# A state-space scan, attention and experts on one core: other scan inputs from ScalarE, softplus in one place, a minimum with an operand per partition

## The chip, the cores and the metric

The kernel runs on one core of a Trainium2 chip. The metric is the time of one execution on the device, in microseconds (us). The time before is the median of three runs. A separate execution was profiled, and the traces and tables below are of that one.

The engines are called by these names: PE (TensorE, with PEld for its weight loads), DVE (VectorE), ACT (ScalarE), POOL (GpSimd) and SP (SyncE, which issues the DMAs).

## The reference

Two layers work on four images of 384 channels by 32 x 32 positions, all in 32-bit floats.

Layer 0 is a selective scan. An image is normalised by groups. For each of four directions `k` (rows, columns, and both reversed) it is projected to a step width `dt`, to `B` and to `C`. Each channel then carries 16 states along the 1024 positions:

```python
dt = jax.nn.softplus(dts.astype(jnp.float32) + dt_projs_bias...[None, :, :, None])
...
dA = jnp.exp(dtt[..., None] * A)
h = h * dA + (dtt * ut)[..., None] * bt[:, :, None, :]
y = jnp.einsum('bkdn,bkn->bkd', h, ct)
```

The four directions are merged and normalised, put through gelu and added to the image.

Layer 1 sees an image as 1024 tokens of 384 channels. A causal attention (softmax of the scores, whose maximum is subtracted) is added. Then a mixture of four experts is added, of which the two likeliest count for each token. The reference computes all four experts, and so does the kernel.

## The kernel before

**Units and ticks.** The scan is cut into 768 units, 192 for each image. A unit holds 32 channels times 4 states on the 128 partitions and 1024 positions along the free dimension. A group is four units (`NJ`) that share their `B` and `C` rows; a block is four groups (`EACH`, 16 units), one direction of 128 channels. The program is written out by a planner, a loop over ticks (lines 1393 to 1422), with one unit a tick. At tick `t` it writes, in this order:

- on ScalarE, the decay `da` of unit `t + 2` (an exponential, line 552; three buffers);
- on VectorE, the scan's input `v = du * B` of unit `t` (`front`, line 559), where it was not made otherwise. `v` lies in PSUM and has two buffers;
- on TensorE, the transposes that make `v` of unit `t + 1` in the other way (`turned`, line 860);
- on POOL, the product of the states of unit `t - 1` with `C` (`back`, line 572), which is ordered behind the VectorE multiply of the same tick;
- work that was put off to this tick, among it `softmax` (line 1008), which stands between the multiply and the scan;
- on VectorE, the scan of unit `t` (`middle`, line 565);
- on TensorE, in every fourth tick, 16 matmuls that sum a group's states into `y` (`row`, line 597);
- DMA loads for units ahead (`fetch`), then one step of the preparation of an image (`preparation`), then the side jobs and as much attention or experts of the image before as a budget allows (`go_on`).

Each engine works through its own queue in this order.

**The other way to a scan input.** In the first image, TensorE and ScalarE are free of attention and experts. There the side job `feed` (lines 776 to 850) prepares the inputs of whole groups. It loads `du` of a block again (line 808). TensorE transposes four 128 x 128 pieces into a PSUM bank (`dut`, line 815), and then the other four. ScalarE copies each piece four times, with a state's `B` as the scale per position (32 instructions a group, line 838), into a buffer `st`. Of these there are two. `turned` transposes back into `v` when the group's units come. A group takes five ticks, eight scalings in each of four. It is left out if it can't be started five ticks before its first unit (`AHEAD`), and a unit whose `st` is not there in time takes the VectorE multiply. A group doesn't start before the one two before it has been consumed (lines 822 to 824). Before the change the second and the fourth group of each block are candidates (line 818).

**Softplus.** `project_dt` (lines 409 to 446) computes `dt` of 128 channels for two directions. In each half of the positions two matmuls fill two PSUM banks, and in a later tick two softplus empty them (line 431). In the first image there are only two such banks, and `feed` uses the same ones. Softplus and the exponential of `da` need different ScalarE tables, so that the change between them is an `ACT_TABLE_LOAD`. Ten such projections fall in the first image's ticks, five for it and five for the second image.

**Softmax.** `scores` makes one or two pieces of 128 rows of scores, already negated, so that the row's minimum `nb` takes the maximum's place. Where there are two pieces, their two minima are combined at line 1016. ScalarE's exponential then reads the result as its bias. `normalise` adds the two exponent sums (line 1028). In each image four of eight row blocks have two pieces.

Of the kernel before, what the change touches and what calls it, by code (L numbers as in the profile page):

```python
# [10 lines left out]
ALU = mybir.AluOpType  # L11
# [22 lines left out]
NQ = N // NI  # L34
NJ = P // DJ
# [7 lines left out]
AHEAD = 5  # L43
# [6 lines left out]
def hybrid_kernel(  # L50
# [22 lines left out]
    nc = tc.nc  # L73
# [37 lines left out]
    clock = [-100]  # L111
# [3 lines left out]
    def defer(ticks, f, where=due):  # L115
        where.setdefault(clock[0] + ticks, []).append(f)
# [176 lines left out]
    def columns(v):  # L293

        return v.rearrange("p (h w) -> p w h", w=HW)
# [113 lines left out]
    def project_dt(b, pair, m, u, xd):  # L409

        ks = PAIRS[pair]
        while not slots.ready(3 + pair):
            yield "wait", 1
        v = u[m]
        if pair == 1:
            v = slots.now(f"ut_{b}_{m}", P, L)
            nc.scalar.copy(v.rearrange("p (w h) -> p w h", h=HW), columns(u[m]))
        dts = [slots.now(f"dt_{b}_{k}_{m}", P, L) for k in ks]
        for h in range(NH):
            while not banks.ready(2):  # L420
                yield "wait", 1
            pss = [banks.now(f"pdt_{b}_{k}_{m}_{h}") for k in ks]
            for i, k in enumerate(ks):
                r = slice(64 * pair + 32 * i, 64 * pair + 32 * i + R)
                nc.tensor.matmul(  # L425
                    pss[i], wdt[r, m * P : (m + 1) * P], xd[r, bass.ts(h, 512)],
                    start=True, stop=True,
                )
            yield "wait", 1
            for i, k in enumerate(ks):  # L430
                nc.scalar.activation(  # L431
                    dts[i][:, bass.ts(h, 512)], pss[i], AF.Softplus, bias=dtb[:, k, m : m + 1]
                )
                banks.give(f"pdt_{b}_{k}_{m}_{h}")
        yield "wait", 1
        for i, k in enumerate(ks):
            nc.sync.dma_start(dts_d[b, k][0, m * P : (m + 1) * P, :], dts[i])
            du = yield from slots.take(f"du_{b}_{k}_{m}", P, L)
            nc.vector.tensor_mul(du, dts[i], v)
            yield "wait", 1  # L440
            nc.sync.dma_start(dts_d[b, k][1, m * P : (m + 1) * P, :], du)
            if b == 0:
                stored_du.add((k, m))
            slots.give(f"dt_{b}_{k}_{m}", f"du_{b}_{k}_{m}")
        if pair == 1:
            slots.give(f"ut_{b}_{m}")

    EACH = NQ * NJ
    IMAGE = M * K * EACH
# [326 lines left out]
    def feed():  # L776
        bt = one.tile([P, 2, NT, 4 * N], F32, tag="fx0", name="bt")

        def turn_rows(pair):
            while pair not in stored_rows:  # L780
                yield "wait", 1
            rows = yield from slots.take(f"bt_{pair}", 4 * N, L)
            nc.sync.dma_start(rows, rows_d[0, pair].rearrange("k j n l -> (k j n) l"))
            yield "wait", 2
            ps = yield from banks.take(f"pbt_{pair}")
            for t in range(NT):
                nc.tensor.transpose(
                    ps[:, t * 4 * N : (t + 1) * 4 * N], rows[:, t * P : (t + 1) * P],
                    ident[: 4 * N, : 4 * N],
                )  # L790
            yield "wait", 1
            nc.scalar.copy(bt[:, pair], ps.rearrange("p (t n) -> p t n", t=NT))
            banks.give(f"pbt_{pair}")
            slots.give(f"bt_{pair}")

        begun = []
        yield from turn_rows(0)
        for n in range(0, IMAGE, EACH):
            u = units[n]
            if clock[0] > n + EACH - NJ - AHEAD:  # L800
                continue
            if u["pair"] == 1 and u["m"] == 0 and u["i"] == 0:
                yield from turn_rows(1)
            while (u["k"], u["m"]) not in stored_du:
                yield "wait", 1
            name = f"turn_{u['name']}"
            du = yield from slots.take(name, P, L)
            nc.sync.dma_start(du, dts_d[0, u["k"]][1, u["m"] * P : (u["m"] + 1) * P, :])
            yield "wait", 2

            def dut(q, h, du=du, name=name):
                ps = banks.now(f"{name}_{q}_{h}")
                for t in range(4):
                    o = (4 * h + t) * P
                    nc.tensor.transpose(ps[:, t * P : (t + 1) * P], du[:, o : o + P], ident)
                return ps

            for q in range(1, NQ, 2):
                n0 = n + q * NJ
                if clock[0] > n0 - AHEAD:  # L820
                    continue
                while len(begun) >= 2 and clock[0] < begun[-2] + NJ:

                    yield "wait", 1
                if clock[0] > n0 - AHEAD:
                    continue
                begun.append(n0)
                st = pools["st"].tile([P, NT, NJ * P], F32, tag="st", name=f"st_{n0}")
                ps = [None, None]
                for h in range(2):  # L830
                    if ps[h] is None:
                        while not banks.ready():
                            yield "wait", 1
                        ps[h] = dut(q, h)
                        yield "wait", 1
                    for t in range(4):
                        for i in range(NI):
                            nc.scalar.activation(  # L838
                                st[:, 4 * h + t, :].rearrange("p (d i) -> p i d", i=NI)[:, i, :],
                                ps[h][:, t * P : (t + 1) * P], AF.Copy,  # L840
                                scale=bt[:, u["pair"], 4 * h + t, u["i"] * 2 * N + q * NI + i :][:, :1],
                            )
                        if t == 1:
                            if h == 0 and banks.ready():
                                ps[1] = dut(q, 1)
                            yield "wait", 1
                    banks.give(f"{name}_{q}_{h}")
                    yield "wait", 1
                scaled[n0] = st
            slots.give(name)  # L850
# [91 lines left out]
    def attention(b, yb, fx0):  # L942
# [65 lines left out]
        def softmax(i, ss, pr):  # L1008
            nb = sm.tile([P, 4], F32, tag="nb", name=f"nb_{b}_{i}")
            if alone:  # L1010
                ps = ss[-1][2][:, -P:]
                nc.vector.tensor_add(ps, ps, causal)
            for n, (o, e, ps) in enumerate(ss):
                nc.vector.tensor_reduce(nb[:, n : n + 1], ps, AX.X, ALU.min)  # L1014
            if len(ss) == 2:
                nc.vector.tensor_tensor(nb[:, 0:1], nb[:, 0:1], nb[:, 1:2], ALU.min)
            for n, (o, e, ps) in enumerate(ss):
                nc.scalar.activation(  # L1018
                    pr[:, o:e], ps, AF.Exp, bias=nb[:, 0:1], scale=-1.0,
                    accum_out=nb[:, 2 + n : 3 + n],  # L1020
                )
                banks.give(f"ss_{b}_{i}_{o}")
            defer(1, lambda: normalise(i, nb, len(ss)))

        def normalise(i, nb, n):
            wd = (i + 1) * P
            if n == 2:
                nc.vector.tensor_add(nb[:, 2:3], nb[:, 2:3], nb[:, 3:4])
            nc.vector.reciprocal(nb[:, 2:3], nb[:, 2:3])
            nc.scalar.activation(prs[i][:, :wd], prs[i][:, :wd], AF.Copy, scale=nb[:, 2:3])  # L1030

# [355 lines left out]
    clock[0] = -2  # L1387
    side.append(later())
    side.append(feed())
    decay(0)  # L1390
    decay(1)
# [85 lines left out]
```

## Time and profile before

| | |
|---|---|
| median of three runs | 3781.38 us (3779.78 to 3781.87) |
| the profiled execution | 3782.19 us, its span 3780.4 us |
| PE busy | 3348.6 us, 89% of the span |
| DVE busy | 2962.4 us, 78% |
| ACT busy | 2088.0 us, 55% |
| POOL busy | 1815.4 us, 48% |
| scans (line 565) | 768, 1750.6 us |
| multiplies for scan inputs (line 559) | 678, 840.6 us |
| scalings for scan inputs (line 838) | 736, 213.6 us |

The span runs from the first instruction to the last. In the slices of the page the span is cut into 40 equal parts of 94.5 us, and a digit is the busy share of a part in tenths. A line of the groups has the source line, engine, operation and tiles, the shapes and the count; then busy us and mean ns of one; then the idle time of the engine before them and what ended it. The busy time counts overlapping instructions once. A line of the timeline has the start and the length in us, the engine, the source line and the operation, with the number of instructions merged in it, and in brackets the idle time before it.

### The profile page before, as it was taken

Reading aid. Unit: us, or ns where it says so; the run is one execution under the profiler, and the core shown is the slowest. Engines: PE = TensorE matmul, PEld = TensorE weight load, DVE = VectorE, ACT = ScalarE, POOL = GpSimd, SP = SyncE. Lnnn points to the kernel's source line nnn. Section 1 sums busy time; section 2 is a strip of 40 time slices with the busy share of each in tenths; the row PEclk is TensorE's granted clock in tenths of the full one; section 3 lists DMA queues with packets and bytes.
Section 4 is the critical chain, followed back from the end, with each engine's and each line's share of the span. In section 5 each row is a group of like instructions: output and inputs, shape, how many; then the busy total and the mean of one; then the engine's idle time right before and its main releaser. Section 6 shows DMA issues by size and latency. Waiting matters only on the chain. (4 is left out here: it accounts for less than half of the span.)

```text
span 3780.4 us, 34707 instructions
## 1 busy us (share of the span) xinstructions
PE 3348.6 (89%) x11755; PEld 1523.6 (40%) x11755; DVE 2962.4 (78%) x2098; ACT 2088.0 (55%) x2754; POOL 1815.4 (48%) x776
## 2 busy tenths in 40 slices
PE   4666666689999999799999999889999998999999
PEld 1333323345343334345333344454344334644444
DVE  5899899988899899989988999999999992210000
ACT  5888888555666556556655555455554552322121
POOL 2777777545466556545555565455665660000000
PEclk7777876799999999898999999899999999999999
DMA  6656555635676757436666655455667551322321
GB/s 202 221 211 223 203 210 200 235 141 177 211 247 210 253 197 245 152 136 219 218 218 227 203 201 197 143 172 196 209 197 241 178 182 38 91 78 81 97 82 53
DMA packets 408017, 680.01 MB, mean 180 GB/s; under 512 B 33520, under 2 KB 279968, under 8 KB 407840
## 3 DMA queue, kind: packets, MB, share of 16 engines
q1 hardware_dynamic: 401632, 677.40, 52.6%
q8 instruction: 93, 1.52, 0.2%
q10 hardware_dynamic: 6208, 0.39, 0.1%
q14 instruction: 84, 0.69, 0.1%
HBM read 605.16 MB, written 72.55 MB: 179 GB/s over the span
## 5 line engine op out<-in xcount | busy, mean ns | idle before, releaser
L572 POOL TENSOR_TENSOR h<-h,bc 128x1024 f32<-128x1024 f32 x768 | 1814.3, 2367 | 1300.8 <-DVE v L559 1170.4
L565 DVE TENSOR_TENSOR_SCAN h<-da,v 128x1024 f32<-128x1024 f32 x768 | 1750.6, 2284 | 107.2 <-PE v L860 31.8
L552 ACT ACTIVATE da<-dt,a 128x1024 f32<-128x1024 f32 x768 | 882.8, 1156 | 916.0 <-DVE h L565 877.8
L1260 PE MATMUL ph<-fx,w 128*128 128x512 f32 x2304 | 1023.3, 600 | 3.5 <-DMA w<-in_w 2.0
L1285 PE MATMUL fy<-ht,w 128*128 128x512 f32 x2304 | 1022.4, 601 | 1.7 <-ACT dt L431 0.9
L559 DVE TENSOR_TENSOR v<-du,bc 128x1024 f32<-128x1024 f32 x678 | 840.6, 1240 | 35.0 <-DMA du<-dts 18.3
L1285 PEld LDWEIGHTS fy<-ht,w 128*128 128x128 f32 x2304 | 437.1, 192 | 575.9 <-issue 558.9
L1260 PEld LDWEIGHTS ph<-fx,w 128*128 128x128 f32 x2304 | 433.8, 191 | 578.6 <-issue 532.8
L597 PE MATMUL y<-h,sel 128*32 128x512 f32 x3072 | 489.7, 659 | 97.4 <-POOL h L572 97.2
L1245 ACT ACTIVATE ht<-ph,b1s 128x512 f32<-128x512 f32 x384 | 257.5, 678 | 463.3 <-PE ph L1260 462.5
L1294 DVE SCALAR_TENSOR_TENSOR fy<-fy,b2s,tw 128x512 f32<-128x512 f32 x96 | 72.4, 754 | 423.0 <-PE fy L1285 423.0
L597 PEld LDWEIGHTS y<-h,sel 128*32 128x32 f32 x3072 | 97.6, 116 | 407.4 <-issue 219.0
L860 PE MATMUL v<-ident,st 128*128 128x128 f32 x720 | 144.2, 366 | 112.7 <-DVE h L565 111.6
L838 ACT ACTIVATE st<-turn,bt 128x128 f32<-128x128 f32 x736 | 213.6, 532 | 0.1
L860 PEld LDWEIGHTS v<-ident,st 128*128 128x128 f32 x720 | 116.1, 190 | 158.3 <-DVE h L565 77.9
L1249 ACT ACTIVATE ht<-ht 128x3072 f32<-128x3072 f32 x64 | 176.9, 2764 | 0.8
L552 ACT ACT_TABLE_LOAD x108 | 138.6, 1283 | 15.5 <-DMA dt<-dts 11.8
L1067 PE MATMUL po<-pt,vt 128*128 128x256 f32 x480 | 110.2, 383 | 10.1 <-ACT pt L959 10.0
L425 PE MATMUL pdt<-xd,wdt 12*128 12x512 f32 x184 | 78.9, 753 | 33.4 <-ACT dt L431 24.7
L997 PE MATMUL ss<-axn,qt 128*128 128x512 f32 (+3 forms) x288 | 101.3, 497 | 7.7 <-ACT yb L1084 6.4
L1067 PEld LDWEIGHTS po<-pt,vt 128*128 128x128 f32 x480 | 96.0, 204 | 27.8 <-ACT pt L959 13.1
L997 PEld LDWEIGHTS ss<-axn,qt 128*128 128x128 f32 x288 | 50.5, 193 | 50.2 <-issue 30.0
(208 smaller groups left out, 1618.3 us busy)
## 6 DMA issues: line engine op xcount, KB each, us to landing
bc<-rows SPq DMA_DIRECT2D x384, 512.0 KB, 4.7
w<-in_w SPq DMA_DIRECT2D x384, 384.0 KB, 5.9
dt<-dts SPq DMA_DIRECT2D x192, 512.0 KB, 3.9
du<-dts SPq DMA_DIRECT2D x192, 512.0 KB, 6.5
dts<-dt SPq DMA_DIRECT2D x48, 512.0 KB, 3.6
dts<-du SPq DMA_DIRECT2D x48, 512.0 KB, 3.8
fx<-t2d SPq DMA_DIRECT2D x12, 768.0 KB, 5.8
tw<-mkd SPq DMA_DIRECT2D x32, 256.0 KB, 6.5
```

What stands on the lines that cost most here:

```text
L552: nc.scalar.activation(u["da"], spread["dt4", n], AF.Exp, scale=a4[:, g, u["q"] : u["q"] + 1])
L559: return nc.vector.tensor_tensor(u["v"], spread["du4", n], spread["bc", n][:, 0, :], ALU.mult)
L565: nc.vector.tensor_tensor_scan(u["h"][:, ::step], u["da"][:, ::step], u["v"][:, ::step], 0.0, op0=ALU.mult, op1=ALU.add,)
L572: product = nc.gpsimd.tensor_tensor(h, h, spread["bc", n][:, 1, :], ALU.mult)
L597: nc.tensor.matmul(y, sel, h, start=first, stop=last, tile_position=(0, jj * DJ))
L838: nc.scalar.activation(st[:, 4 * h + t, :].rearrange("p (d i) -> p i d", i=NI)[:, i, :], ps[h][:, t * P : (t + 1) * P], AF.Copy, scale=bt[ ...
L860: nc.tensor.transpose(u["v"][:, t * P : (t + 1) * P], st[:, t, u["j"] * P : (u["j"] + 1) * P], ident)
L1067: nc.tensor.matmul(pv[:, o:], vt[:, j, m * P : (m + 1) * P], pts[step][j // 4][:, j % 4, o:], start=(alone and j == 0), stop=(j == nj - 1),)
L1245: nc.scalar.activation(ht[:, f, :], ps, AF.Identity, bias=bias)
L1249: nc.scalar.activation(ht, ht, AF.Gelu)
L1260: nc.tensor.matmul(ps, tiles[n][:, c, (f % 2) * P : (f % 2 + 1) * P], xns[h][:, c, :], start=(c == 0), stop=(c == M - 1),)
L1285: nc.tensor.matmul(pss[m], tiles[n][:, f, :], hts[fh][:, f, :], start=(fh == 0 and f == 0), stop=(fh == 1 and f == FH - 1),)
```

## The change

Three edits. In `project_dt`, the wait of a tick between matmuls and softplus is left out for the second half of the positions, in the first image's ticks. In `feed`, all four groups of a block are looked at, and taken are those whose number in the image leaves 1, 3 or 4 when divided by five, in place of every second one. In the attention, two VectorE operations on 128 x 1 tensors take their second operand as a scalar per partition, and no longer as a tensor.

```diff
@@ project_dt
                     start=True, stop=True,
                 )
-            yield "wait", 1
+            if h == 0 or clock[0] >= IMAGE:
+
+                yield "wait", 1
             for i, k in enumerate(ks):
                 nc.scalar.activation(
                     dts[i][:, bass.ts(h, 512)], pss[i], AF.Softplus, bias=dtb[:, k, m : m + 1]
@@ feed
-            for q in range(1, NQ, 2):
+            for q in range(NQ):
                 n0 = n + q * NJ
-                if clock[0] > n0 - AHEAD:
+                if n0 // NJ % 5 not in (1, 3, 4) or clock[0] > n0 - AHEAD:
                     continue
                 while len(begun) >= 2 and clock[0] < begun[-2] + NJ:
@@ softmax
             if len(ss) == 2:
-                nc.vector.tensor_tensor(nb[:, 0:1], nb[:, 0:1], nb[:, 1:2], ALU.min)
+                nc.vector.tensor_scalar_min(nb[:, 0:1], nb[:, 0:1], nb[:, 1:2])
@@ normalise
             if n == 2:
-                nc.vector.tensor_add(nb[:, 2:3], nb[:, 2:3], nb[:, 3:4])
+                nc.vector.tensor_scalar_add(nb[:, 2:3], nb[:, 2:3], nb[:, 3:4])
```

## The prediction

> **What bounds the kernel now.** I read the page's slices first, then the windows by stage, then groups and waits of the first image (60 to 680 us, where nearly all of its 192 scan ticks lie), then single ticks in the timeline.
>
> ```profile
> PE   4666666689999999799999999889999998999999
> DVE  5899899988899899989988999999999992210000
> ACT  5888888555666556556655555455554552322121
> 60.00:680.00 620.00, 393.46 (x1804) 192.47 (x1804) 572.20 (x322) 513.80 (x1044) 450.86 (x190) 0.72 0.60 213
> 1300.00:1500.00 200.00, 198.31 (x613) 80.25 (x616) 182.00 (x126) 112.44 (x115) 111.87 (x48) 0.99 0.64 222
> 2455.00:2520.00 65.00, 54.02 (x251) 31.76 (x250) 63.78 (x58) 34.59 (x60) 32.97 (x14) 0.95 0.35 120
> ```
> The windows' columns are the stretch, its length, busy PE, PEld, DVE, ACT and POOL, then clock and DMA. Image 0 is VectorE's (572 of 620 us); ScalarE has 106 us free there. The experts are TensorE's (198 of 200). A softmax stretch of an attention (the third line) is VectorE's again, 63.8 of 65, and TensorE idles 11 us of it.
>
> Groups and waits of image 0:
>
> ```profile
> L565 DVE TENSOR_TENSOR_SCAN h<-da,v 128x1024 f32<-128x1024 f32 x190 | 429.9, 2281 | 47.4 <-PE v L860 31.8 <-DVE v L559 1.0 <-POOL h L572 0.9
> L838 ACT ACTIVATE st<-turn,bt 128x128 f32<-128x128 f32 x736 | 213.6, 532 | 0.1
> L559 DVE TENSOR_TENSOR v<-du,bc 128x1024 f32<-128x1024 f32 x99 | 126.2, 1275 | 0.3 <-DMA du<-dts 0.3
> L552 ACT ACT_TABLE_LOAD x21 | 26.9, 1283 | 0.4
> L431 ACT ACT_TABLE_LOAD x20 | 25.7, 1283 | 0.3
> ACT da L552 <- DVE h L565: 100.2, 80, 3.6
> ```
> 736 scalings in 32s are 23 groups fed by ScalarE. L559 runs 678 times in the program for 768 units, so 90 units have no VectorE multiply and 102 of image 0's 192 have. VectorE's only real stall is 31.8 us for TensorE's transposes; ScalarE's idling is waiting for VectorE.
>
> One group of each kind:
>
> ```profile
> 302.50 1.33 DVE L559 TENSOR_TENSOR v<-du,bc 128x1024 f32<-128x1024 f32 x1
> 306.17 1.29 DVE L559 TENSOR_TENSOR v<-du,bc 128x1024 f32<-128x1024 f32 x1
> 307.59 8.91 DVE L565 TENSOR_TENSOR_SCAN h<-da,v 128x1024 f32<-128x1024 f32 x4
> 314.01 2.35 PE L597 MATMUL y<-h,sel 128*32 128x512 f32 x16
> 316.30 1.09 PE L860 MATMUL v<-ident,st 128*128 128x128 f32 x8
> 317.52 2.29 DVE L565 TENSOR_TENSOR_SCAN h<-da,v 128x1024 f32<-128x1024 f32 x1 [1.02 <-PE v L860]
> ```
> A multiplied unit comes every 3.6 us (3.67 here). Scans whose input ScalarE and TensorE made follow each other every 2.2. The fourth unit of such a group is late by 1.02, because its transposes stand in TensorE's queue behind the 16 matmuls of the group before.
>
> The softmax on VectorE, beside POOL:
>
> ```profile
> 825.13 2.35 POOL L572 TENSOR_TENSOR h<-h,bc 128x1024 f32<-128x1024 f32 x1 [1.68 <-DVE v L559]
> 825.79 1.71 DVE L1016 TENSOR_TENSOR nb<-nb 128x1 f32<-128x1 f32 x1
> 827.53 0.69 ACT L1018 ACTIVATE pr<-ss,nb 128x512 f32<-128x512 f32 x1 [1.79 <-DVE nb L1016]
> 843.23 0.23 DVE L340 TENSOR_SCALAR gn_mc<-gn_mc 128x3 f32<-128x3 f32 x1
> 3220.22 0.16 DVE L1016 TENSOR_TENSOR nb<-nb 128x1 f32<-128x1 f32 x1
> ```
> The minimum of two numbers a partition takes 1.71 us and ends at 827.50, 0.02 after POOL's product (827.48). With POOL idle, in the last image, it takes 0.16. The twelve of the first three attentions hold VectorE for 16.43 us (windows for this line alone).
>
> [...] L340 ends at 843.46, 0.02 after POOL's product (841.10, 2.34 long). [...] Eight transposes take 1.97 us at 309.93 and 1.09 at 316.30, right behind 16 matmuls[...].
>
> **The change part by part.** *Which groups.* Of image 0's 48 groups, 28 have a number that leaves 1, 3 or 4 by 5. By the planner's rules a group is prepared in 5 ticks from its start; it may not start before the group two before it is consumed (two st buffers), nor while softplus or the projection holds both PSUM banks, nor until two ticks after its du was asked for; and it must start 7 ticks ahead for all four units to be in time. Applied to before they give 23 groups and 90 units, as the trace has it. Applied to the new order they drop group 1 (too early) and group 4 (its du is asked for at tick 10, so 12, past its limit of 11). The other 26 start 7 to 12 ticks ahead, the second of every pair 7 or 8. So 104 units, 14 more.
>
> *VectorE.* A multiplied group is 3.54+3.60+3.67+3.63 = 14.45 us from tick to tick, a fed one 2.20+2.24+2.20+2.26 = 8.90 (starts of the scans of ticks 72 to 79 in the timeline) plus the stall of its fourth unit. 14 units at (14.45-8.90)/4 = 1.39 are -19.4 us. Stalls: 26 groups at 1.05 (the 1.02 above; 31.8 over 23 groups is 1.4, some of it softplus) are 27.3. Ten groups now begin inside a fed group, and four transposes of theirs (0.60, the row of L815 in the timeline) come ahead of a late fourth unit: +6. The softplus of tick 44 stands inside a fed group, ahead of its transposes: +2.2 (its matmuls end some 4.6 after a scan: da 1.15, load 1.28, softplus 1.3, matmul 0.9; transposes 2.0 more; VectorE would be ready after two fed ticks, 4.4; the others stand in multiplied groups or at a fed group's end). Together 35.5 against 31.8, +3.7. Image 0: **-15.7, rounded to -15**. Both ends: -19.4[...] (1.07 instead of 1.97 for eight transposes), -3 if each of the 8 pairs loses 1.5 more.
>
> *ScalarE.* Three groups more at 213.6/23 = 9.3 are +28. Standing together, ten softplus of two halves lose one load to softplus and one back each: -20 x 1.283 = -25.7. But the second half's matmul now waits for the first half's softplus to free its bank, and ScalarE stands in its queue for it: about 0.9 (one matmul of 753 ns and the hand-over), +9. Sum +11: 525 of some 605, 87%. I cost it at nothing; its cover is the wait of 100.2. Behind the waiting softplus stands the next decay (da), which VectorE needs two ticks later, so 0.9 is inside that lead. If the cover were gone the whole +11 would show.
>
> *Moved steps.* Each softplus hands on its dt and du one tick earlier (four stores on SP's queue, now ahead of one tick's loads of dt, du and bc; two multiplies of 1.25 on VectorE), and the reloads of du for the transposes come at other ticks, still one per block of four groups. None is late now: VectorE's wait for du is 0.3 us. POOL does the same 192 products at 2.37, 455 us, below the span.
>
> *Minimum and sum.* [...] the twelve fall from 16.43 to 12 x 0.16 = 1.9: -14.5 on VectorE. In those stretches VectorE sets the pace and TensorE idles about 10 us per stretch, so most reaches the end; I take three quarters, **-11** (from -5 to -14.5). [...] The sum of two exponent sums (L1028, 0.13, POOL idle) gains nothing; +0.03 at worst by the row of tensor_scalar, 16 times: nothing.
>
> *Sum.* Nothing after image 0 waits for a fixed time; both engines enter image 1 earlier by the same amount. The profiled execution took 3782.2 (its span 3780.4 and 1.8 around it): 3782.2 - 15 - 11 = **3756**. The shown median, 3781.4, lies 0.8 below it; I let that stand.
>
> **Rivals.**
> - *The minimum still blocks*, as L340 did: 3782.2 - 15 = 3767. For it: each of the three L340 that begins beside a product ends with it. Against it: they are three elements wide.
> - *Image 0 gives nothing*: TensorE becomes the bound inside the pairs (its transposes, 16 matmuls and du transposes come to about 20 us of a pair's 20[...]) and eats 15 us; with the minimum free 3771, without it 3782. Against it: 393 busy of 620[...].
> - *Slower: ScalarE falls behind in the pairs.* A tick with eight scalings costs it 3.05 us (da starts at 110.25, 113.28 and 116.31 in its timeline), a fed tick costs VectorE 2.2. Four such ticks fall in each of 8 pairs: 4 x 0.85 x 8 = 27, and then softplus' stalls (+9) show too. Against the 15 gained that is +21: 3792 with the minimum free, 3803 with it blocked. It decides once the lead of two ticks (4.4 us in fed ticks) is used up, and VectorE then waits for da. Against it: a pair's other four ticks cost 1.15 each, so a pair needs 4 x 3.05 + 4 x 1.15 = 17 of 20 us.
>
> **How the numbers follow.** Forecast 45% (its own range 3746 to 3764), minimum blocked 30%, image 0 nothing 15% (two thirds of it with the minimum free), slower 10%. The range leaves out the slower case and the top of the third, and takes -19.4 and -14.5 at its foot, with 2 for the spread of the runs shown: 3746 to 3776. About 0.2%, 7.6 us, is what a measurement can tell from no change. Faster: 45 + 30 + 5 = 80%; same 10% (the third's 3782, and half of its 3771, which lies close to the bound of 3774); slower 10%.
>
> **What would show it.** 832 scalings and 664 multiplies of L559; ten fewer table loads each at L431 and L552 before 680 us; image 0's last scan some 15 us earlier; L1016 at 0.16 beside POOL or again ending with it. Wrong if scans wait for da, if the wait for PE at the scans passes 50 us, or if later images' ticks, whose banks and slots shift a little, move by more than image 0 gains.

## The result, and the profile after

Median 3768.8 us (3763.9 to 3775.0) against 3781.4 in the kernel before: ratio 0.9966, interval [0.9957, 0.9975], 12.6 us faster. The profiled execution took 3767.4, its span 3765.6. The forecast was 3756, with a range of 3746 to 3776: the direction was right, the size half of what was forecast.

The window of the first image in the changed kernel:

```profile
60.00:680.00 620.00, 409.02 (x1951) 203.93 (x1952) 572.12 (x314) 508.93 (x1122) 454.40 (x192) 0.74 0.61 219
```

VectorE is as full in 60 to 680 us as it was (572.1 against 572.2), although that stretch now holds 12 multiplies for scan inputs fewer (87, before 99) and only two scans more. Groups of the same stretch:

```profile
L567 DVE TENSOR_TENSOR_SCAN h<-da,v 128x1024 f32<-128x1024 f32 x192 | 432.9, 2279 | 34.7 <-PE v L862 20.2 <-PE y L599 1.6 <-POOL h L574 1.3
L840 ACT ACTIVATE st<-turn,bt 128x128 f32<-128x128 f32 x832 | 244.1, 556 | 0.1
L433 ACT ACTIVATE dt<-pdt,dtb 128x512 f32<-128x512 f32 x40 | 25.4, 684 | 18.6 <-PE pdt L425 18.5
L441 DVE TENSOR_TENSOR du<-dt,x 128x1024 f32<-128x1024 f32 x10 | 18.1, 1806 | 3.7 <-ACT dt L433 3.7
L554 ACT ACT_TABLE_LOAD x11 | 14.1, 1283 | 0.2
L561 DVE TENSOR_TENSOR v<-du,bc 128x1024 f32<-128x1024 f32 x87 | 113.4, 1303 | 3.7 <-DMA du<-dts 3.4 <-DMA bc<-rows 0.2
```

and two of them in the kernel before:

```profile
L431 ACT ACTIVATE dt<-pdt,dtb 128x512 f32<-128x512 f32 x40 | 25.3, 683 | 1.0 <-PE pdt L425 0.7
L439 DVE TENSOR_TENSOR du<-dt,x 128x1024 f32<-128x1024 f32 x10 | 12.7, 1272 | 0.0
```

The list of VectorE's waits between 60 and 720 us (total, times, longest):

```profile
DVE h L567 <- PE v L862: 20.2, 24, 2.5
DVE du L441 <- ACT dt L433: 7.2, 8, 2.0
```

832 scalings and half the table loads are there as forecast (11 loads of 1283 ns at the decays and 10 at softplus in this stretch, before 21 and 20). Scans wait less for TensorE's v (20.2 us, before 31.8). Three costs are new: ScalarE waits 18.5 us for the second matmuls of a projection (0.7 before), VectorE waits 7.2 for softplus (none in image 0 before), and ten of the 20 multiplies that make du (those of the row directions) take 1806 ns on average instead of 1272. A tick is called fed here when its scan's input came from ScalarE and TensorE, and multiplied when VectorE made it.

The timeline shows why three of the ten take longer. In a fed tick nothing orders POOL's product behind a du multiply:

```profile
94.36 6.98 POOL L574 TENSOR_TENSOR h<-h,bc 128x1024 f32<-128x1024 f32 x3 [1.26 <-DVE v L561]
99.07 3.36 DVE L441 TENSOR_TENSOR du<-dt,x 128x1024 f32<-128x1024 f32 x1 [0.28 <-ACT dt L433]
```

The last of the three products joined in the first line began 0.09 before the multiply and ends at 101.34; the multiply stands until then and ends 1.09 later. A du multiply in a fed tick isn't new: seven of the 20 lay in one before, and none took over 1.28. They didn't wait for softplus and began 0.16 to 0.22 ahead of their tick's product, as this one of the kernel before:

```profile
107.10 1.20 DVE L439 TENSOR_TENSOR du<-dt,x 128x1024 f32<-128x1024 f32 x1
107.26 3.27 POOL L572 TENSOR_TENSOR h<-h,bc 128x1024 f32<-128x1024 f32 x1 [1.94 <-DVE h L565]
```

There it is POOL's product that takes 3.27 instead of 2.36. In the changed kernel the three multiplies that are held for over 1 us (at 99.07, 209.46 and 648.29) had each waited for softplus just before, and began 0.08 to 0.81 after the product.

And the minimum:

```profile
819.54 2.36 POOL L574 TENSOR_TENSOR h<-h,bc 128x1024 f32<-128x1024 f32 x1 [1.70 <-DVE v L561]
820.20 0.21 DVE L1018 TENSOR_SCALAR nb<-nb 128x1 f32<-128x1 f32 x1
```

It takes 0.21 in the middle of POOL's product, which before held it until 0.02 after its own end.

How much later each scan starts than in the kernel before (negative is earlier; worked out from the scans' starts in the traces; the starts of the programs themselves differ by up to 1.8):

| tick | after | minimum alone | groups and softplus, old minimum |
|---|---|---|---|
| 0, first scan | -1.3 | -1.8 | -1.4 |
| 192, image 0 done | -7.6 | -2.3 | -6.1 |
| 204 | -5.6 | -2.3 | -4.1 |
| 236, first attention done | -11.0 | -7.3 | -4.5 |
| 290 | -16.8 | -8.5 | -10.7 |
| 300, first experts done | -8.6 | -8.5 | -2.7 |
| 767, last scan | -14.7 | -14.9 | -2.7 |

From its first scan to the first of image 1, image 0 took 626.3 us, before 632.6: it gained 6.3, not 15. By tick 300 the changed kernel has no more lead than the one with the new minimum alone, and its whole time is 1.5 us better (3768.8 against 3770.3), which the intervals don't tell apart.

Each of these figures is from one trace. Kernels whose image 0 is the same give 632.6, 632.1 and 635.0 (before, minimum alone, and the two-column minimum below) and 626.3 and 627.9 (changed, and changed with the old minimum), so a difference of under some 3 us in image 0 isn't told from none.

### The profile page after: what moved, and what is told of

Its sections match the earlier page's. It is cut to its first block, busy times and chain, and to the rows that moved or that the text cites. A ratio compares the mean times of both kernels' runs of the same rounds, so it can differ in the third digit from the quotient of the medians.

```text
span 3765.6 us, 35032 instructions
## 1 busy us (share of the span) xinstructions
PE 3357.1 (89%) x11891; PEld 1530.6 (41%) x11891; DVE 2942.4 (78%) x2084; ACT 2085.1 (55%) x2832; POOL 1815.9 (48%) x776
## 5 line engine op out<-in xcount | busy, mean ns | idle before, releaser
L567 DVE TENSOR_TENSOR_SCAN h<-da,v 128x1024 f32<-128x1024 f32 x768 | 1748.8, 2283 | 94.3 <-PE v L862 20.2
L561 DVE TENSOR_TENSOR v<-du,bc 128x1024 f32<-128x1024 f32 x664 | 824.9, 1242 | 44.0 <-DMA du<-dts 22.3
L840 ACT ACTIVATE st<-turn,bt 128x128 f32<-128x128 f32 x832 | 244.1, 556 | 0.1
L554 ACT ACT_TABLE_LOAD x99 | 127.0, 1283 | 15.0 <-DMA dt<-dts 11.6
L425 PE MATMUL pdt<-xd,wdt 12*128 12x512 f32 x184 | 86.9, 799 | 45.8 <-ACT dt L433 23.1
L433 ACT ACTIVATE dt<-pdt,dtb 128x512 f32<-128x512 f32 x92 | 58.3, 683 | 21.6 <-PE pdt L425 21.2
```

The costliest lines, as they stand in the source:

```text
L554: nc.scalar.activation(u["da"], spread["dt4", n], AF.Exp, scale=a4[:, g, u["q"] : u["q"] + 1])
L561: return nc.vector.tensor_tensor(u["v"], spread["du4", n], spread["bc", n][:, 0, :], ALU.mult)
L567: nc.vector.tensor_tensor_scan(u["h"][:, ::step], u["da"][:, ::step], u["v"][:, ::step], 0.0, op0=ALU.mult, op1=ALU.add,)
L840: nc.scalar.activation(st[:, 4 * h + t, :].rearrange("p (d i) -> p i d", i=NI)[:, i, :], ps[h][:, t * P : (t + 1) * P], AF.Copy, scale=bt[ ...
```

## Experiments

**One edit at a time.** My theory before the runs: the groups give most of their 17 us, the joined softplus takes much of it back on VectorE, and the minimum gives some 7 to 10. Three kernels take the edits apart.

The minimum alone (the kernel before, with the two softmax lines of the change):

> The minimum and the sum of the score statistics take their second operand per partition; groups and softplus stay as before. Theory 1 (the minimum is freed from POOL, and the expert stages that TensorE sets give part of it back): each minimum 0.21 us instead of 1.2 to 1.9 beside POOL, the scans after the third attention 11 to 13 us earlier than before, the end 7 to 10 us earlier, about 3773. Theory 2 (all of it reaches the end): 12 to 14 us, about 3768. Theory 3 (its time is waited for elsewhere): within 2 us of before. Under every theory image 0 is unchanged.

3770.3, ratio 0.9969 [0.9958, 0.9980], 11.3 us faster. The minima take 0.21 each, 13.9 us less of VectorE in twelve; the last scan is 13.1 earlier, measured from the first. Theory 3 falls. Theory 1's place in the attentions is right, but the expert stages gave nothing back before the last scan; the 11.3 lie between the ends of theories 1 and 2, and the interval (7.6 to 15.9) reaches into both.

The other two edits, without the minimum (and the sum, likewise put back):

```diff
-                nc.vector.tensor_scalar_min(nb[:, 0:1], nb[:, 0:1], nb[:, 1:2])
+                nc.vector.tensor_tensor(nb[:, 0:1], nb[:, 0:1], nb[:, 1:2], ALU.min)
```

> The changed kernel with the old minimum and sum: the groups of five and the joined softplus alone. Theory 1: image 0 ends 5 to 8 us earlier than before, less than the 16.9 us of multiplies that go, because the du multiplies and their waits take some 10 back; end 3 to 6 us earlier than before, about 3777. Theory 2 (the two edits feed on each other, image 0 helps the attentions): the end as after, 3769. Theory 3 (TensorE's stages swallow what image 0 gains): within 2 us of before.

3779.8, ratio 0.9994 [0.9986, 1.0003]: not to be told from no change. At the end of image 0 it stood 6.1 ahead, as theory 1 said (1.4 of them already at its first scan: image 0 itself took 627.9, before 632.6); of the end theory 3 was right.

The softplus alone (the kernel before, with the condition on the tick's wait):

> Only the softplus of a projection stands together; groups by the old rule, minimum as before. Theory 1 (joined softplus moves cost onto VectorE): the table loads of image 0 fall by about ten and ScalarE by some 13 us, yet nothing is gained: the du multiplies wait 4 to 8 us for their softplus and stand beside POOL's product for some us more, so 0 to 6 us slower than before, 3781 to 3787. Theory 2 (ScalarE's loads are on the path of the fed scans): waits of the scans for v fall from 31.8 us to under 25, 3 to 8 us faster, 3774 to 3779.

3790.4, ratio 1.0027 [1.0018, 1.0036], 8.9 us slower: theory 1's direction, and more than its 6. Image 0 takes 642.6, ten more than before. The largest new item on VectorE there isn't softplus (3.6 us of waits) but waiting for loads of du and of the B and C rows: 9.8 us, before 2.2.

**The groups with softplus apart.** The reverse, with projections 11 ticks apart instead of 12, since otherwise the second image's preparation ends too late:

```diff
-            if h == 0 or clock[0] >= IMAGE:
+            if True:
 
                 yield "wait", 1
...
-                yield "wait", 0 if b == 0 and m == 0 else 12
+                yield "wait", 0 if b == 0 and m == 0 else 11
```

> The changed kernel with softplus apart as before (a tick between its halves) and the projections one tick closer, so that the second image's preparation still ends in time: groups of five by the new rule (about 101 units fed) and the new minimum. Theory 1 (the joined softplus takes back what the groups give): the du multiplies stay near 1.3 us, no wait for softplus, image 0 ends 10 to 14 us earlier than before instead of 7.6, end about 3764. Theory 2 (the groups need the joined softplus, ScalarE would be late with them): the scans wait over 35 us for v in image 0, which ends less than 5 us earlier, end about 3772 or more.

3767.8, ratio 0.9959 [0.9945, 0.9973]. Neither theory as a whole: the du multiplies are clean (1.20 to 1.29 in image 0), as theory 1 said, but image 0 takes 629.3, only 3.3 less than before. The list of waits (50 to 679 us) has the largest item:

```profile
DVE h L567 <- PE v L862: 33.3, 23, 4.1
```

That is 13.1 more than in the changed kernel, though only 1.5 more than in the kernel before. VectorE's waits for loads are 8.2, before 2.2.

So alone the softplus costs 10 in image 0, the groups bring about 3 (with 101 fed units and closer projections; hardly more than two traces of one kernel differ by), and both together bring 6.3 in one trace and 4.7 in the other. Beside the softplus edit the groups are worth 15 to 16, the amount that I forecast for them.

**VectorE's own losses removed.** If the collisions and the wait for softplus were the cost, their removal had to pay. First, POOL's product of a fed tick ordered behind that tick's du multiply:

```diff
-            nc.vector.tensor_mul(du, dts[i], v)
+            multiplied[:] = [clock[0], nc.vector.tensor_mul(du, dts[i], v)]
...
+        if after is None and multiplied[0] == n:
+            after = multiplied[1]
         product = nc.gpsimd.tensor_tensor(h, h, spread["bc", n][:, 1, :], ALU.mult)
```

> The changed kernel, with POOL's product of a fed tick ordered behind the du multiply of that tick, so that the multiply doesn't stand still until the product is through. Theory 1 (the collisions cost what they last): du multiplies all at 1.2 to 1.3 us, 6.5 us of excess gone, the wait for softplus stays near 7; image 0 ends about 4 to 6 us earlier than in the changed kernel, the whole at about 3764. Theory 2 (the product that starts 1.25 us later is late in its turn, for y or for the next multiply): no gain, 3767 to 3771.

3767.0, ratio 0.9957 [0.9945, 0.9970]. The collisions are gone (0.5 us of 6.5 left), yet image 0 takes 625.9 instead of 626.3. By the whole's time both theories are near; image 0, which theory 1 had 4 to 6 shorter, speaks for no gain. Whether the product was late in its turn, theory 2's reason, stays open.

Then the du multiplies a tick later:

```diff
                 banks.give(f"pdt_{b}_{k}_{m}_{h}")
-        yield "wait", 1
+        yield "wait", 2
...
-                yield "wait", 0 if b == 0 and m == 0 else 12
+                yield "wait", 0 if b == 0 and m == 0 else 11
```

> The changed kernel with the du multiplies one tick later behind the joined softplus, and the projections one tick closer so that the second image's preparation ends as before. Theory 1 (the multiplies came a tick too early): the wait of 7.2 us for softplus goes to under 1, some of the collisions stay; image 0 ends 4 to 9 us earlier than in the changed kernel, the whole at 3761 to 3766. Theory 2 (the du loads behind them are then late): waits for du loads grow from 3.4 to over 7 us, no gain, 3767 to 3772.

3773.1, ratio 0.9974 [0.9965, 0.9984]. The wait for softplus is gone and so are most collisions (0.9 left), 12.8 us of VectorE together; image 0 takes 624.8, only 1.5 less. The waits for du loads (3.9) haven't grown as theory 2 had it. What came instead is in the list of waits (60 to 720 us):

```profile
DVE h L567 <- PE v L862: 29.6, 28, 3.9
DVE v L561 <- DMA du<-dts: 3.9, 3, 1.5
DVE h L567 <- ACT da L554: 3.1, 3, 1.8
```

The place can be seen in one tick. In the changed kernel's timeline, around a projection inside a fed group:

```profile
205.90 1.26 ACT L433 ACTIVATE dt<-pdt,dtb 128x512 f32<-128x512 f32 x2
206.64 2.65 PE L425 MATMUL pdt<-xd,wdt 12*128 12x512 f32 x4 [0.85 <-ACT dt L433]
208.74 1.27 ACT L433 ACTIVATE dt<-pdt,dtb 128x512 f32<-128x512 f32 x2 [1.58 <-PE pdt L425]
209.46 2.62 DVE L441 TENSOR_TENSOR du<-dt,x 128x1024 f32<-128x1024 f32 x1 [0.89 <-ACT dt L433]
209.48 1.12 PE L817 MATMUL turn<-ident,turn 128*128 128x128 f32 x4 [0.20 <-ACT dt L433]
210.39 1.91 PE L862 MATMUL v<-ident,st 128*128 128x128 f32 x8
212.41 2.29 DVE L567 TENSOR_TENSOR_SCAN h<-da,v 128x1024 f32<-128x1024 f32 x1 [0.33 <-PE v L862]
```

and the same scan with the later du multiplies:

```profile
206.78 1.92 PE L862 MATMUL v<-ident,st 128*128 128x128 f32 x8
208.83 2.29 DVE L567 TENSOR_TENSOR_SCAN h<-da,v 128x1024 f32<-128x1024 f32 x1 [3.86 <-PE v L862]
```

The wait of 0.89 and the collision of 1.4 lay inside a chain of other engines: softplus, the second matmuls, softplus, turn, and only then the transposes for the next scan. Without them the scan waits 3.86 for the same transposes: from the scan before to this one it is 6.12 us in the changed kernel and 6.15 here. In the whole kernel this run is slower than the changed one. Its lead shrinks from 13.9 at tick 300 to 10.2 at the last scan, while the changed kernel's grows from 8.6 to 14.7. Both the later multiplies and the closer projections reach the later images. The run with softplus apart has the closer projections alone and gains nothing there either (10.7 and 10.9), so they may be the cause; no run separates the two.

Both at once:

> Both: the du multiplies one tick later, and POOL's product of a fed tick behind them. Theory 1: neither wait nor collision is left, image 0 ends 9 to 12 us earlier than in the changed kernel, about the 15 that the multiplies promise against the kernel before; the whole at 3757 to 3761. Theory 2 (what is saved is waited for at TensorE, 20 us of waits for v grow to 30): 3764 to 3769.

3774.8, ratio 0.9980 [0.9972, 0.9989], image 0 625.2, waits for v 31.4. Theory 1, that VectorE's own losses are what image 0 lacks, has fallen: the three runs moved image 0 by at most 1.5, where this one was to move it by 9 to 12. I formed theory 3: a projection's tick is set by the chain above, in which v stands behind turn.

**Turn a tick later.** The second half's banks are given back one tick after its softplus:

```diff
-                banks.give(f"pdt_{b}_{k}_{m}_{h}")
-        yield "wait", 1
+                if h == 0:
+                    banks.give(f"pdt_{b}_{k}_{m}_{h}")
+        late = 1 if clock[0] < IMAGE else 0
+        yield "wait", late
+        banks.give(*[f"pdt_{b}_{k}_{m}_1" for k in ks])
+        yield "wait", 1 - late
```

> The changed kernel, with the two banks of a projection's second half given back one tick after its softplus, so that the transposes of a du block (turn) go into TensorE's queue a tick later, behind the transposes that make the next fed unit's v. About 101 units are fed instead of 104 (3 more multiplies, some 3.5 us against it). Theory 3 (the length of a projection's tick is the chain table load, softplus, second matmuls, softplus, turn, v, in which v stands behind turn; VectorE's own waits and collisions lie inside it): the time lost around the ten projections falls from 9 to 3 to 5 us, image 0 ends 1 to 3 us earlier than in the changed kernel in spite of the 3 units, the whole at 3765 to 3768. Theory 1 (VectorE's collisions and waits for softplus are the cost): unchanged around the projections, the three units are lost, 3771 to 3773.

> The same with the du multiplies a tick later and the projections two ticks closer (about 97 units fed, 7 more multiplies, some 8 us against it). Theory 3: with v no longer behind turn and no du multiply waiting, the time lost around the projections is under 3 us; image 0 ends 1 to 3 us later than in the run with the held banks alone, for the units that it lacks: 3767 to 3771. Theory 1: the waits for v around the projections come back as in the run with the later du multiplies, 8 us there: 3776 to 3781.

> The held banks, and POOL's product of a fed tick behind the du multiply. Theory 3: once v isn't behind turn, a collision of a du multiply costs again what it lasts, and its removal is worth 3 to 5 us: 3761 to 3765. Theory 1 says the same of the collision but no gain of the banks: 3766 to 3768. If the collisions remain covered by something else, as in the changed kernel: within 1.5 us of the run with held banks alone.

3769.4 (0.9962 [0.9949, 0.9974]), 3777.3 (0.9986 [0.9979, 0.9992]) and 3771.0 (0.9970 [0.9958, 0.9982]). By the whole's time the second is where theory 1 had it, and the other two fit neither theory. To estimate the time lost around projections I subtract from each tick what it needs undisturbed (2.35 fed, 3.72 multiplied, 1.27 for a du multiply) and add up the ticks from a projection's first softplus to three behind its last: 2.0 us before, 10.5 in the changed kernel, 12.2 with the softplus alone. With held banks it is 6.1, in the other two 14.1 and 8.1. With four ticks behind instead of three the changed kernel has 16.5 and held banks 12.4, so the estimate is rough. It is a smaller fall than theory 3 asked for, and image 0 takes 630.2, 644.7 and 633.4; of the 3.9 that the first of them is longer than the changed kernel, the three units account for some 3.4. No gain of the new order of turn and v is left. It isn't a clean test of that order: moving the banks moved the groups, and waits for v came at other ticks (46.3 us of idle time before the fed scans in the second, before 33.5).

**ScalarE relieved.** Last, the chain's table loads taken out, on top of the later du multiplies. This kernel leaves softplus out, so it serves for the time alone:

```diff
-                    dts[i][:, bass.ts(h, 512)], pss[i], AF.Softplus, bias=dtb[:, k, m : m + 1]
+                    dts[i][:, bass.ts(h, 512)], pss[i],
+                    AF.Softplus if clock[0] >= IMAGE else AF.Exp, bias=dtb[:, k, m : m + 1]
```

> The changed kernel with the later du multiplies, and in the projections within image 0 Exp in place of Softplus: Softplus is left out there, and with it 20 table loads of 1.28 us (25.7 us of ScalarE) disappear; VectorE, TensorE, the queues and the order of everything stay as in the run with the later du multiplies, in which image 0 took 624.2 us from the first scan to the first of image 1. Theory 3 (a projection's tick is as long as ScalarE's chain with TensorE behind it): the waits for v (29.6 us) and for da (3.1 us) fall by 8 to 15 us, image 0 takes 610 to 617 us, the whole at 3758 to 3765. Theory 1 (VectorE's own work and collisions set image 0): the waits for v fall by under 3 us, image 0 takes 621 to 625 us, the whole within 3 us of 3773.

3765.6, ratio 0.9956 [0.9939, 0.9972]; image 0 620.2, 4.6 less than the 624.8 with the loads (the expectation says 624.2), between the two theories; the waits for v fall by 3.2, from 29.6 to 26.4. The scan shown above now waits less, but still waits for the same thing:

```profile
203.75 1.27 ACT L433 ACTIVATE dt<-pdt,dtb 128x512 f32<-128x512 f32 x2 [2.09 <-PE pdt L425]
207.45 2.29 DVE L568 TENSOR_TENSOR_SCAN h<-da,v 128x1024 f32<-128x1024 f32 x1 [2.95 <-PE v L863]
```

Two loads of 1.28 left the tick, one of them ahead of the transposes, and the scan's wait fell by 0.91; the second softplus then waits 2.09 for its matmuls instead of 1.58. So a load is part of the chain in this tick, but of 25.7 us of ScalarE only 4.6 came out of image 0.

**What frees the minimum.** The kernel before with two columns in place of one:

```diff
-                nc.vector.tensor_tensor(nb[:, 0:1], nb[:, 0:1], nb[:, 1:2], ALU.min)
+                nc.vector.tensor_scalar_min(nb[:, 0:2], nb[:, 0:2], nb[:, 1:2])
```

> The kernel before with the minimum over two columns and an operand per partition (the second column isn't read). Theory 1[...]: 0.2 us whether POOL runs or not. Theory 2 (only one element per partition escapes[...]): it ends with POOL's product, 1.2 to 1.9 us, as in the kernel before. With theory 1 about 3770, with theory 2 about 3781.

Its timeline:

```profile
826.04 2.34 POOL L572 TENSOR_TENSOR h<-h,bc 128x1024 f32<-128x1024 f32 x1 [1.68 <-DVE v L559]
826.70 1.71 DVE L1016 TENSOR_SCALAR nb<-nb 128x2 f32<-128x2 f32 x1
```

Theory 2. With two elements per partition the operation is held as the old minimum was: the one shown takes 1.71 and ends 0.03 after POOL's product, and the sixteen take 1004 ns on average, against 214 for the single element in the run with the minimum alone. So among the three forms that ran, the operand per partition didn't free it with two elements, and the single element didn't free it with two tensors as operands (the old minimum); the form with both ran free. What sets the difference isn't shown. This kernel ran once, at 3786.9, so its time isn't compared.

No version here is measurably faster than the changed kernel: the intervals of the best, at 0.9956 to 0.9959, overlap its own.

## Why the prediction was half right

The ticks of image 0 by kind, added up from the records (191 ticks, from the first scan to image 0's last; the last column runs on to the first scan of image 1; the idle time is VectorE's):

| | fed ticks | mean of one | multiplied ticks | mean of one | idle | image 0 |
|---|---|---|---|---|---|---|
| before | 90 | 2.70 | 101 | 3.82 | 49.9 | 632.6 |
| after | 104 | 2.65 | 87 | 3.99 | 50.2 | 626.3 |
| softplus alone | 92 | 2.68 | 99 | 3.96 | 54.3 | 642.6 |
| groups, softplus apart | 101 | 2.81 | 90 | 3.80 | 56.9 | 629.3 |
| product behind du | 104 | 2.64 | 87 | 4.00 | 55.8 | 625.9 |
| du later | 104 | 2.71 | 87 | 3.90 | 56.0 | 624.8 |
| du later, no loads | 104 | 2.68 | 87 | 3.88 | 51.6 | 620.2 |

And VectorE's time in these ticks by item, where it changed:

| us | before | after |
|---|---|---|
| multiplies for scan inputs | 128.5 | 113.3 |
| waits of scans for v from TensorE | 31.8 | 20.2 |
| du multiplies | 23.7 | 29.5 |
| waits for softplus | 0 | 7.2 |
| waits for loads | 2.2 | 6.0 |
| group norm, with its wait | 1.2 | 4.7 |
| waits of scans for y | 0 | 1.6 |

- *Which groups.* 26 groups, 104 units, 664 multiplies: as worked out.
- *VectorE, 14 units.* The forecast was -15.7, and fourteen ticks at 3.82 - 2.70 are 15.8 (unrounded means). That agreement is arithmetic on the kernel before, and the parts came out otherwise: the multiplies gave 15.2, and the stalls of fed scans fell by 11.6 where I added 3.7. The end of -19.4 took eight transposes at 1.07 throughout the pairs, which was my estimate from single ones in the trace. For the second groups it nearly came true: eight transposes take 1.05, 1.09, 1.30 and 1.04 us on average for the four units of a pair's second group, and 1.67, 1.86, 1.73 and 1.09 for those of the other groups. In five of the eight second groups the last scan waits 0.24. Together that is more than the term forecast, and most of it was taken back.
- *ScalarE, +11, costed at nothing, and moved steps, "None is late now".* Here the step failed. The sum itself was near (ScalarE 4.9 us less busy, and 17.8 more of waits for a projection's matmuls), but it wasn't free. The round trip to TensorE took 18.5/10 = 1.85 per projection, not 0.9, and the du multiplies came to stand behind it: 7.2 of waits for softplus, 5.8 of longer du multiplies. And the loads were late: 3.8 more (the longest wait, 2.71, at 116.64 us for du). Per tick, the 87 multiplied ones cost 0.16 more each, 14.0 us; the fed ones gave 4.6 back; the 9.4 between them are what is missing from 15.7. The softplus alone, 10 us slower in image 0, is the measurement of what I had put at zero.
- But those items aren't the cost one by one. Removing 6.0 and 12.8 us of them took 0.4 and 1.5 from image 0. I gave the other engines' work a cover of 100 us of waiting. That wait is a sum over 80 ticks; in the projection's tick shown above ScalarE has no wait between 204.60 and 212.37 but the 1.58 for TensorE, so the cover isn't there. With softplus apart the price shows in the fed ticks instead (2.81).
- *Minimum.* 11 forecast, 11.3 measured alone, with 13.9 off VectorE (forecast 14.5): the minimum runs free beside POOL's product, at 0.21. That an operand per partition would free it was my estimate; nothing in the trace before showed it. It gives nearly all of the 12.6. The share that reaches the end was taken at three quarters without a sum, and came out at four fifths.
- *"Nothing after image 0 waits for a fixed time".* Wrong as well. Of a lead of 5.3 us over the kernel with the minimum alone at tick 192, 2.0 are lost by tick 204, where VectorE waits 1.7 for ScalarE's rs_l (a wait that the kernel before doesn't have there). In the first experts the lead swings: the changed kernel loses what is left of it at the 5.0 below, misses the wait of 6.0 that the kernel before has at 951.91 us and is 8.3 ahead at tick 290, and loses that in one wait of 7.4 at 1145.30. The lists of waits from 880 to 1180 us, changed kernel and then kernel before:

```profile
DVE du L441 <- PE fy L1287: 7.4, 1, 7.4
DVE sc L1120 <- PE pgate L1113: 5.0, 1, 5.0
```

```profile
DVE du L439 <- PE ph L1260: 6.8, 2, 6.0
```

TensorE is busy for 97 to 99 of every 100 us there in the changed kernel. The other runs agree: seven kernels lead the one with the minimum alone by 1.4 to 11.9 us at tick 192, and none by more than 3.1 at tick 330. So the minimum's gain passes through this stage and image 0's lead doesn't; that much is shown. Why TensorE didn't end earlier with its earlier start isn't settled.

By the number alone the first rival, a minimum that still blocks (3767), lies nearest to the result, and the trace rules it out: the minimum takes 0.21. The second, image 0 gives nothing with the minimum free (3771), is nearest to what happened at the end, though not by TensorE being the bound inside the pairs. What stays open is what keeps image 0 near 625 us whatever VectorE saves: which part of the chain of ScalarE and TensorE, or the loads, for which VectorE waits 5.5 to 7.7 us in each of the runs with 104 fed units and the new minimum (2.2 before). No run tested the loads.

## What to carry to other kernels

Two edits that look independent may not add up: here one alone cost 10 us of image 0, the other alone gave about 3, and both gave 5 to 6. Run each alone before adding. When an engine's waits and collisions lie inside a longer chain of other engines, removing them can move the wait and not the end, as it did here; look at what else ends in the same tick before charging them. A gain early in a program may be lost in a later stage that another engine sets: here 5.3 us of image 0 became 1.5 at the end.

## What the runs showed of the hardware

In the changed kernel the minima of one element per partition with an operand per partition took 212 to 215 ns, eleven of the first twelve beside POOL's product and the other five without it. In the kernel before, with two tensors as operands, the first twelve took 0.67 to 1.71 us and each ended 0.01 to 0.02 after the product beside it; the four of the last image, with no product beside them, took 0.16. With two elements and an operand per partition the one shown took 1.71 and ended 0.03 after the product. The group norm's subtraction of 128x3 took 2375 ns in one fed tick of the changed kernel, ending 0.02 after POOL's product, and 163 in the kernel before. Of a 128x1024 du multiply on VectorE and POOL's product, the one that began later took longer in the cases shown: the multiply took 3.36 instead of 1.20 us where it began 0.09 after the product, and the product 3.27 instead of 2.36 where it began 0.16 after the multiply. The eight 128 x 128 transposes of a unit took 1.05 to 1.30 us on average in a fed group that followed another, and 1.67 to 1.86 in the first three units of the others.
